# Allocation order and buffer counts: FFN weights and activations at equal addresses modulo 256

## The chip, the cores and the metric

The kernel runs on one core of a Trainium2 chip. The metric is the device time of one execution in microseconds (us); lower is better. Three runs of the kernel before gave 479.50, 479.63 and 480.22 us.

## The reference

One pre-norm transformer layer in fp32, on x of 4 batches x 512 rows x 512 columns:

```python
x = x + attn(layernorm(x), W_q, W_kv, W_o)
x = x + ffn(layernorm(x), gate_w, up_w, down_w, gate_scale, up_scale, down_scale)

# attn: q = x @ W_q.T, kv = x @ W_kv.T, 16 heads of 32
#   qf, kvf = fft over the 32 of a head, each divided by its norm
#   kvf = cumsum(kvf) over the rows;  out = ifft(qf * kvf).real @ W_o.T
# ffn: w -> float8_e4m3 and back for the three weights
#   f = silu((x @ gate_w) * gate_scale) * ((x @ up_w) * up_scale)   # 1536 wide
#   out = (f @ down_w) * down_scale                                  # 512 wide
```

## The kernel before

The order of instructions is written out by hand: each engine runs its instructions in the order of the source, and no scheduler moves them. Tiles come from pools; a pool lays its tiles down in the order in which they are first asked for, so this order and the sizes and buffer counts of earlier tiles set every later tile's address.

**Attention, about 0 to 204 us.** The 2048 rows are 16 chunks of 128. The Fourier transforms are folded into the weights at the start (`fold_in`, `fold_out`). For each chunk TensorE makes the two spectra (pq, L302), a running sum over the rows with a triangle of ones (cum, L357) and the output projection (po, L397). Spectra and projection are full fp32 matmuls. The running sum takes F32R operands, which TensorE handles in one pass: the value is split into a high part kh and a low part kl, and both are multiplied with tri_r and added up. `stats` (L250 to L260) makes mean and 1/deviation of 128 rows with ScalarE and GpSimd, in small tiles "less" (4 buffers) and "dev" (6 buffers). Beside all this ScalarE, VectorE (DVE) and GpSimd (POOL) round the FFN's weights to the float8 grid, a unit of 128 x 1024 at a time (`quant_*`, L196 to L225), into wg, wu and wd.

**FFN, about 204 us to the end.** It has 48 steps: 4 batches x 12 blocks of 128 inner columns. A step n has two parts:

- `inner(n)`, L458 to L485: the gate's 8 and the up's 8 one-pass matmuls into gu (L465). Loaded weights (lhsT) are a 128-column block of wg or wu; the moving operand is 512 columns of yh (high part of the normalized rows) or yl (low part). For each of 4 blocks k, yh and then yl use the same weights. Then ScalarE, DVE make f = silu(gate) * up and split it into fh and fl, which lie in the buffers of kh and kl.
- `down(n - 1)`, L487 to L511: 8 one-pass matmuls into pd (L498). Loaded weights are 128 columns of fh or fl of the step before, the moving operand is 512 columns of wd.

In `behind(n)` stand the remaining weight roundings (first batch alone) and the next batch's rows: statistics, normalization, a turn through DRAM and DVE (`y_turn`, L441 to L452) into the next yh and yl. On the SP queue stand the loads of x, the raw weights, the DRAM turns and the output; ScalarE's queue carries one small transfer per chunk ("row").

The tiles that the change and the prediction speak of, with their byte offset in each partition before and after, and its remainder modulo 256:

| tile | before | mod 256 | after | mod 256 |
|---|---|---|---|---|
| nhalf (64 bytes) | 18624 | 192 | 18656 | 224 |
| table (4 bytes) | 92928 | 0 | 18624 | 192 |
| gus (96 bytes) | 92960 | 32 | 18720 | 32 |
| tri_r | 18688 | 0 | 18816 | 128 |
| wg | 19200 | 0 | 19328 | 128 |
| wu | 43776 | 0 | 43904 | 128 |
| wd | 68352 | 0 | 68480 | 128 |
| dsc | 93056 | 128 | 93056 | 128 |
| yh, yl, wkv, wq, wo (pool "big") | 95104 + 8192 i | 128 | 95104 + 8192 i | 128 |
| x, z, xT, t | from 152448, 2048 apart | 128 | the same | 128 |
| kh, fh (3 buffers) | 187840 + 2048 i | 192 | 188032 + 2048 i | 128 |
| kl, fl (3 buffers) | 193984 + 2048 i | 192 | 194176 + 2048 i | 128 |
| qvT | 220864 | 192 | 221056 | 128 |

A tile of 4 bytes takes 32. All steps inside these tiles (128 columns of fp32 are 512 bytes, 512 columns are 2048) are multiples of 256, so each operand of a matmul has its tile's remainder. Modulo 512 the weights wg, wu, wd lie at 256 before and at 384 after, yh and yl at 384 in both, and fh and fl at 448 before and at 128 after.

Of the kernel before, what the change touches and what calls it, by code (L numbers as in the profile page):

```python
# [7 lines left out]
F32 = mybir.dt.float32  # L8
I32 = mybir.dt.int32
F32R = mybir.dt.float32r  # L10
AF = mybir.ActivationFunctionType
# [4 lines left out]
P = 128  # L16
# [14 lines left out]
def tile_fft_attention_then_fp8_ffn(  # L31
# [38 lines left out]
    nc = tc.nc  # L70
# [4 lines left out]
    MC = FF // P  # L75
# [4 lines left out]
    const = ctx.enter_context(tc.tile_pool(name="const", bufs=1))  # L80
    big = ctx.enter_context(tc.tile_pool(name="big", bufs=7))
    work = ctx.enter_context(tc.tile_pool(name="work", bufs=2))
# [43 lines left out]
    nc.gpsimd.memset(eps, EPS)  # L126
    over = const.tile([P, 1], F32, name="over")
    nc.gpsimd.memset(over, -E4M3_OVERFLOW * DOWN * HUGE)
    nhalf = const.tile([P, H], F32, name="nhalf")
    nc.gpsimd.memset(nhalf, -0.5)  # L130
    tri_r = const.tile([P, P], F32R, name="tri_r")

    wg = const.tile([P, KC, FF], F32R, name="wg")
    wu = const.tile([P, KC, FF], F32R, name="wu")
    wd = const.tile([P, MC, D], F32R, name="wd")

    table = const.tile([P, 1], F32, name="table")
    nc.gpsimd.memset(table, 0.0)
    nc.scalar.activation(table, table, AF.Silu)
    y_all = dram.tile([B, TC, P, D], F32, name="y_all")  # L140
    xn_all = dram.tile([B, TC, P, D], F32, name="xn_all")

# [107 lines left out]
    def stats(src, name):  # L250

        less = work.tile([P, 1], F32, tag="less", name=f"less_{name}", bufs=4)
        rstd = work.tile([P, 1], F32, tag="dev", name=f"dev_{name}", bufs=6)
        each = work.tile([P, D], F32, tag="end", name=f"each_{name}", bufs=1)
        nc.scalar.activation(each, src, AF.Identity, accum_out=less)
        nc.scalar.activation(less, less, AF.Copy, scale=-1.0 / D)
        nc.scalar.activation(each, src, AF.Square, bias=less, accum_out=rstd)
        nc.scalar.activation(rstd, rstd, AF.Identity, scale=1.0 / D, bias=eps)
        nc.gpsimd.tensor_tensor(rstd, rstd, nhalf[:, 0:1], ALU.pow)
        return less, rstd  # L260
# [24 lines left out]
    def x_stats(i):  # L285
        st_x[i] = stats(xt[i], nm(i))
# [128 lines left out]
    def y_stats(b, c):  # L415
        st_y[b, c] = stats(ys[b][:, c, :], f"f{b}_{c}")
# [143 lines left out]
    norms(0, 0)  # L560
    next_parts(1, True)

    gus = const.tile([P, 2, MC], F32, name="gus")
    dsc = const.tile([P, D], F32, name="dsc")
    nc.sync.dma_start(gus[:, 0, :], gate_scale)
    nc.sync.dma_start(gus[:, 1, :], up_scale)
# [185 lines left out]
```

## Time and profile before

| what | value |
|---|---|
| median of 3 runs | 479.63 us |
| the profiled execution | 479.59 us |
| its span on the core | 477.8 us |
| granted TensorE clock, mean | 0.999 |
| weight loads, L302, L465 and L498 | 188 to 190 ns each |
| gu matmuls, L465 | 4 groups of 192 |
| pd matmuls, L498 | 2 groups of 192 |
| DVE busy, 213.8 to 252.8 us | 34.06 of 39.00 us |

How to read it: PE is TensorE's matmuls and PEld its weight loads, which run beside the matmuls before them. A matmul's recorded duration is modelled and reaches past the next one's start, so that the duration of a group's mean (391 to 403 ns for L465) is not what a matmul costs in a row; the distance from one start to the next is. A full fp32 matmul of 512 columns stands in the trace as two records. The page's groups give busy time, mean duration, and the idle time ahead of the group with what ended it. The wait view lists who waited for whom. The timeline gives each instruction's start and duration in us.

### The profile page before, as it was taken

What the parts mean: (1) busy time and instruction counts of PE and PEld (TensorE: products, weight loads), DVE (VectorE), ACT (ScalarE), POOL (GpSimd) and SP (SyncE); (2) the same over time, 40 slices, a digit from 0 to 9 for tenths busy, and PEclk for the clock granted to TensorE, in tenths of its full rate; (3) what the DMA queues carried; (4) which work ended last, traced back from release to release, by engine and by line L of the source; (5) the groups of instructions that cost most, each with busy time, mean ns of one, the idle gap of its engine ahead of it and who ended that gap; (6) DMA issues with size and microseconds to landing.
All of it is one profiled execution on the core that took longest, in us unless ns stands there. A gap on an engine that the chain in (4) does not pass through costs nothing.

```text
span 477.8 us, 5013 instructions
## 1 busy us (share of the span) xinstructions
PE 465.8 (98%) x1736; PEld 314.3 (66%) x1736; DVE 285.8 (60%) x399; ACT 214.8 (45%) x418; POOL 200.9 (42%) x134
## 2 busy tenths in 40 slices
PE   6999999999999999999999999999999999999995
PEld 6534444444444444668888888888888888888883
DVE  1558998888998788768899352333433332522225
ACT  3556475656555864414752325533226433222220
POOL 0247999997987886531432140122210021400002
PEclk9999999999999999999999999999999999999999
DMA  8920414242451200524241040430041420200002
GB/s 277 359 68 24 155 66 155 91 143 93 140 175 58 75 22 22 177 88 154 45 111 22 1 174 3 98 79 0 22 156 37 94 47 0 89 0 1 0 0 88
DMA packets 46152, 40.72 MB, mean 85 GB/s; under 512 B 27696, under 2 KB 28080, under 8 KB 46128
## 3 DMA queue, kind: packets, MB, share of 16 engines
q1 hardware_dynamic: 45744, 40.39, 26.8%
q8 instruction: 13, 0.21, 0.2%
q14 instruction: 11, 0.09, 0.1%
q10 hardware_dynamic: 384, 0.03, 0.1%
HBM read 28.85 MB, written 11.53 MB: 85 GB/s over the span
## 4 chain that ended last, share of the span: by engine, by line
PE 77%; DVE 9%; ACT 5%; POOL 4%; DMA 3%; issue 2%; SPq 0%; DVEq 0%; ACTq 0%
PE gu L465 37%; PE pd L498 19%; PE pq L302 12%; PE po L397 6%; POOL rn L323 3%; DMA row<-end 2%; PE pkv L150 1%; PE pt_v L271 1%; ACT sq L313 1%; ACT end L364 1%; DVE ss L318 1%; DVE qm L217 1%; PE pw L165 1%; PE cum L357 1%; DVE qa L221 1%
## 5 line engine op out<-in xcount | busy, mean ns | idle before, releaser
L323 POOL TENSOR_TENSOR rn<-ss,nhalf 128x16 f32<-128x16 f32 x32 | 107.4, 3358 | 22.3 <-DVE ss L318 22.3
L478 DVE SCALAR_TENSOR_TENSOR f<-gu,gus,g 128x512 f32<-128x512 f32 x48 | 36.0, 750 | 113.7 <-PE gu L465 112.1
L465 PE MATMUL gu<-yh,wg 128*128 128x512 f32 x192 | 77.4, 403 | 0.0
L465 PE MATMUL gu<-yh,wu 128*128 128x512 f32 x192 | 76.6, 399 | 0.0
L498 PE MATMUL pd<-wd,fl 128*128 128x512 f32 x192 | 75.5, 393 | 0.0
L465 PE MATMUL gu<-yl,wu 128*128 128x512 f32 x192 | 75.4, 393 | 0.0
L498 PE MATMUL pd<-wd,fh 128*128 128x512 f32 x192 | 75.3, 392 | 0.0
L465 PE MATMUL gu<-yl,wg 128*128 128x512 f32 x192 | 75.1, 391 | 0.0
L481 ACT CAST fh<-f 128x512 fp32r<-128x512 f32 x48 | 29.8, 621 | 90.7 <-DVE f L478 90.7
L302 PE MATMUL pq<-wkv,xT 128*128 128x512 f32 x128 | 57.7, 594 | 0.6 <-DVE xT L294 0.6
L397 PE MATMUL po<-wo,qvT 128*128 128x512 f32 x128 | 57.6, 593 | 0.0
L302 PE MATMUL pq<-wq,xT 128*128 128x512 f32 x128 | 57.6, 592 | 0.0
L476 ACT ACTIVATE g<-gu,gus 128x512 f32<-128x512 f32 x48 | 33.0, 687 | 54.4 <-PE gu L465 53.6
L510 POOL TENSOR_TENSOR o<-o,ys 128x512 f32<-128x512 f32 x14 | 17.7, 1295 | 83.2 <-DVE o L508 83.2
L483 DVE TENSOR_TENSOR fl<-f,fh 128x512 fp32r<-128x512 f32 x48 | 35.4, 737 | 26.9 <-ACT fh L481 26.8
L302 PEld LDWEIGHTS pq<-wkv,xT 128*128 128x128 f32 x128 | 24.1, 190 | 30.4 <-issue 27.0
L465 PEld LDWEIGHTS gu<-yh,wg 128*128 128x128 f32 x192 | 36.0, 188 | 9.5 <-issue 0.5
L465 PEld LDWEIGHTS gu<-yh,wu 128*128 128x128 f32 x192 | 36.0, 188 | 9.3
L498 PEld LDWEIGHTS pd<-wd,fl 128*128 128x128 f32 x192 | 36.0, 188 | 8.7 <-DVE fl L483 0.2
L465 PEld LDWEIGHTS gu<-yl,wg 128*128 128x128 f32 x192 | 36.1, 188 | 8.4 <-issue 0.5
L498 PEld LDWEIGHTS pd<-wd,fh 128*128 128x128 f32 x192 | 36.0, 188 | 8.3
L465 PEld LDWEIGHTS gu<-yl,wu 128*128 128x128 f32 x192 | 36.1, 188 | 8.0
(84 smaller groups left out, 598.5 us busy)
## 6 DMA issues: line engine op xcount, KB each, us to landing
x<-in_x SPq DMA_DIRECT2D x16, 256.0 KB, 2.8
xT<-in_xT SPq DMA_DIRECT2D x16, 256.0 KB, 2.7
y_all<-x SPq DMA_DIRECT2D x16, 256.0 KB, 2.0
ys<-y_all SPq DMA_DIRECT2D x4, 1024.0 KB, 6.3
out<-o SPq DMA_DIRECT2D x16, 256.0 KB, 2.0
rawf<-in_gate_w SPq DMA_DIRECT2D x3, 1024.0 KB, 6.5
rawf<-in_up_w SPq DMA_DIRECT2D x3, 1024.0 KB, 5.3
rawf<-in_down_w SPq DMA_DIRECT2D x3, 1024.0 KB, 6.2
```

The lines of the kernel that those rows point to most:

```text
L150: nc.tensor.matmul(pw[i][:, j * P : (j + 1) * P], lhsT=r[:, j, i * P : (i + 1) * P], rhs=fwd, start=True, stop=True,)
L165: nc.tensor.matmul(pw, lhsT=inv, rhs=r[:, j, :], start=True, stop=True)
L302: nc.tensor.matmul(pq, lhsT=xTs[i][:, k, :], rhs=w[:, k, :], start=k == 0, stop=k == KC - 1)
L323: nc.gpsimd.tensor_tensor(rns[i, j], sss.pop((i, j)), nhalf, ALU.pow)
L397: nc.tensor.matmul(po, lhsT=qvT[:, k, :], rhs=wo[:, k, :], start=k == 0, stop=k == KC - 1)
L465: nc.tensor.matmul(p, lhsT=w[:, k, m * P : (m + 1) * P], rhs=v[:, k, :], start=k == 0 and v is yhs[b], stop=k == KC - 1 and v is yls[b],)
L476: nc.scalar.activation(g, pgu[0], AF.Silu, scale=gus[:, 0, m : m + 1])
L478: nc.vector.scalar_tensor_tensor(f, pgu[1], gus[:, 1, m : m + 1], g, ALU.mult, ALU.mult)
L481: nc.scalar.copy(fh, f)
L483: nc.vector.tensor_tensor(fl, f, fh.bitcast(F32), ALU.subtract)
L498: nc.tensor.matmul(pds[b][c], lhsT=v[:, c * P : (c + 1) * P], rhs=wd[:, m, :], start=m == 0 and v is fused[n][0], stop=m == MC - 1 and v i ...
L510: add.tensor_tensor(o, o, ys[b][:, c, :], ALU.add)
```

## The change

Three edits in the allocation, none in the computation:

- `table`, the operand of an activation whose use is to load ScalarE's Silu table, is allocated and filled ahead of nhalf instead of behind the weights;
- `gus`, the two scale vectors of the gate and the up matmul, is allocated ahead of tri_r and the weights instead of behind the attention's first chunks; the two DMAs that fill it stay where they were;
- the tag "dev" of `stats` gets 12 buffers instead of 6.

No instruction is added or removed. On GpSimd the fills of table and nhalf change places; on the other engines and on the SP queue the order is the same. With 12 buffers, some of the ScalarE and GpSimd instructions of `stats` (L257, L259) no longer carry a wait for an older reader of their buffer.

```diff
     over = const.tile([P, 1], F32, name="over")
     nc.gpsimd.memset(over, -E4M3_OVERFLOW * DOWN * HUGE)
+
+    table = const.tile([P, 1], F32, name="table")
+    nc.gpsimd.memset(table, 0.0)
+    nc.scalar.activation(table, table, AF.Silu)
     nhalf = const.tile([P, H], F32, name="nhalf")
     nc.gpsimd.memset(nhalf, -0.5)
+
+    gus = const.tile([P, 2, MC], F32, name="gus")
     tri_r = const.tile([P, P], F32R, name="tri_r")
 
     wg = const.tile([P, KC, FF], F32R, name="wg")
     wu = const.tile([P, KC, FF], F32R, name="wu")
     wd = const.tile([P, MC, D], F32R, name="wd")
-
-    table = const.tile([P, 1], F32, name="table")
-    nc.gpsimd.memset(table, 0.0)
-    nc.scalar.activation(table, table, AF.Silu)
...
-        rstd = work.tile([P, 1], F32, tag="dev", name=f"dev_{name}", bufs=6)
+        rstd = work.tile([P, 1], F32, tag="dev", name=f"dev_{name}", bufs=12)
...
-    gus = const.tile([P, 2, MC], F32, name="gus")
     dsc = const.tile([P, D], F32, name="dsc")
     nc.sync.dma_start(gus[:, 0, :], gate_scale)
     nc.sync.dma_start(gus[:, 1, :], up_scale)
```

## Prediction

> **What bounds the kernel now.** I read the page's busy shares and its chain of waits first, then the groups by cost, then TensorE's own waits in the second half, and last the timeline of single matmuls.
>
> ```profile
> PE 465.8 (98%) x1736; PEld 314.3 (66%) x1736; DVE 285.8 (60%) x399; ACT 214.8 (45%) x418; POOL 200.9 (42%) x134
> ...
> PE 77%; DVE 9%; ACT 5%; POOL 4%; DMA 3%; issue 2%; SPq 0%; DVEq 0%; ACTq 0%
> PE gu L465 37%; PE pd L498 19%; PE pq L302 12%; PE po L397 6%; POOL rn L323 3%; DMA row<-end 2%; PE pkv L150 1%; PE pt_v L271 1%; ACT sq L313 1%; ACT end L364 1%; DVE ss L318 1%; DVE qm L217 1%; PE pw L165 1%; PE cum L357 1%; DVE qa L221 1%
> ```
>
> TensorE is the engine of the chain, and two lines of it, gu (L465) and pd (L498), are 56% of the span. Those are the FFN's one-pass (F32R) matmuls, 768 and 384 of them. The wait view for TensorE from 200 us on says whether anything else holds them up:
>
> ```profile
> engine line waited for: us in total, times, longest us
> PE cum L357 <- ACT g L476: 0.2, 1, 0.2
> ```
>
> Nothing does: from about 204 to 472 us TensorE goes from one matmul to the next. So what counts is the spacing from start to start. The timeline (start, duration) around the end of one FFN step and the start of the next:
>
> ```profile
> 263.31 0.39 PE L498 MATMUL pd<-wd,fh 128*128 128x512 f32 x1
> 263.55 0.39 PE L498 MATMUL pd<-wd,fl 128*128 128x512 f32 x1
> 263.77 0.40 PE L465 MATMUL gu<-yh,wg 128*128 128x512 f32 x1
> 264.00 0.39 PE L465 MATMUL gu<-yl,wg 128*128 128x512 f32 x1
> 264.23 0.40 PE L465 MATMUL gu<-yh,wg 128*128 128x512 f32 x1
> 264.47 0.39 PE L465 MATMUL gu<-yl,wg 128*128 128x512 f32 x1
> ...
> 267.27 0.39 PE L465 MATMUL gu<-yl,wu 128*128 128x512 f32 x1
> 267.50 0.39 PE L498 MATMUL pd<-wd,fh 128*128 128x512 f32 x1
> ```
>
> The durations overlap, so they say little; the starts are what to read. Sixteen gu take 263.77 to 267.50, 3.73 us, which is 233 ns each. The trace's start times, in whole ns, show more. In the gu run the spacing alternates 237, 229, 237, 229. At the end of the kernel, where 24 pd follow each other, it repeats 232, 226, 229 (mean 229). The pd that is followed by a gu takes 226 or 227 (263.55 to 263.77 above), in nearly all 44 pairs of that kind that stand in full flow.
>
> For comparison, a record of the attention's full fp32 matmuls (L302, L397) starts every 429 ns. Each is recorded as two, so it is four times 214.5. A one-pass matmul therefore loses 12 to 23 ns somewhere.
>
> **What the Trainium skill says.** "TensorE: Matmul & The Clock Gate", section Back-to-back issue gap, gives N/2.4 + 2.5 ns for a warm matmul, 216 ns at 512 columns. The fp32 records agree (429 / 2 = 214.5), the one-pass matmuls don't (226 to 238, granted clock 1.00). The same page, section Step-by-step, says of the weight load that it "doesn't steal SBUF read bandwidth from the running matmul". And "SBUF — State Buffer", section Who interferes with whom, lets TensorE wait for nobody. The trace speaks against both as far as they go: spacing varies while the weight load beside it stays at 188 ns. No page ties the spacing to addresses, so what follows rests on the trace.
>
> **Where the addresses come in.** The weights that load during a matmul are those of the next one (the weight load's record starts 2 to 4 ns after the matmul). I take each matmul's moving address, the address of the next weights, and their difference modulo 256, from the table of addresses ahead. Within a gu run it is 128. Within a pd run it is 192. From the last gu to the first pd it is 64, and from the last pd to the first gu it is 0, since wd and wg both lie at 0. So the trace already has one kind of matmul with equal addresses, and it is the 226 to 227 one.
>
> A second thing sets the spacing. Start times modulo 13.33 ns are far from evenly spread, and for one difference the spacing is nearly a function of that remainder. For difference 128: remainder 1 to 2 gives 237, remainder 12 gives 229, and each leads to the other, which is the alternation. To compare fairly I take matmuls that start at the same remainder, 9.5 to 10.5: difference 0 gives 226 to 227 (44 matmuls), difference 128 gives 234 (47), difference 192 gives 234 to 237 (47). And 226.7 is 17 times 13.33, so a matmul of difference 0 that starts there ends there: a run of them would stay at 226.7. That it holds for a whole run is my step, as no run of them stands in the trace.
>
> **The change, part by part.**
>
> - *Addresses of the FFN's matmuls.* With gus ahead of the weights, table in front of nhalf and six more small stats buffers, wg, wu, wd, yh, yl, kh, kl all lie at 128 modulo 256: all differences become 0. An FFN step is 16 gu and 8 pd, 3.73 + 1.85 = 5.574 us by start times. At 226.7 it is 24 x 226.7 = 5.441 us, 0.133 less. Times 48 steps: 6.4 us.
>  Bounds for this unknown: the floor is 214.5 for each, 24 x 214.5 = 5.148, -0.426 x 48 = -20.4 us. The other end is that every matmul takes the dearest steady value, 237.5: 24 x 237.5 = 5.700, +0.126 x 48 = +6.0 us. I take -6.4.
> - *Running sum (L357).* 32 one-pass matmuls move from difference 64 to 0 (tri_r and kh, kl). At most 10 ns each, 0.3 us, and partly on the chain only: nothing taken.
> - *fp32 matmuls.* qvT moves from 192 to 128, wo stays at 128. L302 (equal all along) and L397 (unequal before) both have 429 ns, so nothing.
> - *Other engines' operands* move from 192 to 128 as well. ScalarE's cast 128x512 takes 621 ns on f (at 192, L481) and 620 on t (at 128, L451): nothing.
> - *Stats buffers 6 to 12.* Some waits of L257 and L259 for an old reader go away. In ScalarE's and GpSimd's wait views no such wait is among those that cost time: nothing. Nothing is added that could wait.
> - *table ahead of nhalf.* GpSimd's fills are 0.1 us at 0.77 and 0.82 us. ScalarE's table load runs from 0.72 to 2.00 whatever they do, and nhalf is first read at 8.13. Nothing. The queues' order is otherwise the same, DMAs of gus included.
>
> **What is late next.** A faster TensorE comes sooner to what DVE and GpSimd make. The last wu quantization starts at 243.4 and takes at most 1.7; the m = 8 step that reads it starts at 247.2 and gets to those rows 12 matmuls later, 250.0. The last wd ends by 260.8 and is read at 267.7. The next batch's last yl ends at 267.7 and is read at 269.5. By then TensorE is ahead by 10 x 0.133 = 1.3 us, so 1.8 shrinks to 0.5 even if GpSimd kept its clock time; its work follows TensorE's steps, so it mostly moves along. If that cover were gone, it would cost a few tenths once. DVE is at 34.06 of 39.00 us in that stretch and would be at 34.06 of 38.1. The tail after the last pd (471.6 to 477.8: DVE, GpSimd, output DMA) stays.
>
> **Sum.** The profiled execution took 479.59 us: span 477.8 and 1.8 around it. The median of the runs is 479.63, the same. 479.6 - 6.4 = 473.2.
>
> **Rivals.**
>
> 1. *Less: equal means modulo 512.* gu gets difference 0 modulo 512, as in the pair above; pd gets 256 modulo 512, which no F32R pair of the trace has. The nearest is kl of the running sum ahead of po (difference 256, next weights fp32): 226 to 235, mean 232, no better than pd today. Then only gu gains: 16 x (233.1 - 226.7) x 48 = 4.9 us, 474.7; with a worse pattern for gu, 475 to 478.6.
> 2. *More.* The 0-pair is followed by 234 and 224 where 237 and 229 would stand, so part of its gain may show in its neighbours: 5 + 8 = 13 ns in all. If each matmul gained 13 from 233, it would take 220: 24 x 220 = 5.280, 14.1 us less, 465.5. For: two matmuls of unchanged difference are faster after it. Against: that shift follows from the remainder they start at.
> 3. *Nothing happens.* Spacing is the 188 ns weight load plus a fixed 40, whatever the addresses: 479.6. For: the weight load never varies. Against: spacing does, 224 to 238, beside the same weight load.
> 4. *Slower.* Runs of equal addresses don't settle at remainder 10 but in a cycle at the dear end, as gu's remainder 1 to 2 shows 237. The place is the gu and pd runs, the price up to +6.0 us (485.6); it decides from a settled mean above 232.2 ns (5.574 / 24). Against: the only equal pairs are the cheapest at their remainder, and lead back to it.
>
> **How the numbers follow.** Forecast, 472 to 475: 0.42. Rival 1 outside that, 475 to 478.6: 0.20. Rival 2, 465 to 472: 0.18; below 465, towards the floor: 0.04. Nothing: 0.06. Slower: 0.10. A measurement of this kernel can tell about 0.2% (1 us) from no change. Faster by more: 0.84; within: 0.06; slower: 0.10. The range from 465.0 to 478.6 holds 0.80.
>
> **What would show it.** Right: gu and pd spacing near 227 with little alternation, an FFN step of 5.44 us, first half and tail as they were, weight load still 188. Rival 1: gu at 227 and pd at 229 to 232. Rival 2: spacing near 220. Rival 3: 237/229 unchanged. Rival 4: a mean above 232. New entries in TensorE's wait view after 204 us would say that another engine has taken over, which would make the prediction wrong with its spacing right.

## The result and the profile after

The changed kernel takes 473.44 us (median of 4 runs, 472.47 to 474.62) against 479.56 us before, a ratio of 0.9874 with a 95% interval of 0.9846 to 0.9903. The profiled execution took 473.83 us with a span of 471.8 us, 6.0 less than before. Lines of the code are two further down: gu is L467, pd is L500.

From the page of the changed kernel, the busy shares and two lines of the chain:

```profile
PE 459.6 (97%) x1736; PEld 314.4 (67%) x1736; DVE 285.8 (61%) x399; ACT 214.8 (46%) x418; POOL 200.9 (43%) x134
...
PE 77%; DVE 8%; ACT 7%; DMA 3%; issue 3%; POOL 2%; SPq 0%; DVEq 0%; ACTq 0%
PE gu L467 36%; PE pd L500 18%; PE pq L304 12%; PE po L399 6%; DMA row<-end 2%; ACT sq L315 1%; POOL rn L325 1%; PE pkv L152 1%; PE pt_v L273 1%; ACT end L366 1%; PE pw L167 1%; ACT qa L212 1%; DVE kn L328 1%; PE cum L359 1%; DVE kn L342 1%
```

Instruction counts and the busy time of DVE, ScalarE, GpSimd and of the weight loads are the same to 0.1 us. Only the time of TensorE's matmuls shrank, by 6.2 us. Its wait view from 200 us on still shows no one else holding it up:

```profile
PE cum L359 <- ACT g L478: 0.5, 1, 0.5
```

The timeline at the same place as before, the end of one FFN step and the start of the next (start, duration):

```profile
262.75 0.39 PE L500 MATMUL pd<-wd,fl 128*128 128x512 f32 x1
262.97 0.39 PE L467 MATMUL gu<-yh,wg 128*128 128x512 f32 x1
263.20 0.39 PE L467 MATMUL gu<-yl,wg 128*128 128x512 f32 x1
263.42 0.39 PE L467 MATMUL gu<-yh,wg 128*128 128x512 f32 x1
263.65 0.39 PE L467 MATMUL gu<-yl,wg 128*128 128x512 f32 x1
...
266.37 0.39 PE L467 MATMUL gu<-yl,wu 128*128 128x512 f32 x1
266.60 0.39 PE L500 MATMUL pd<-wd,fh 128*128 128x512 f32 x1
266.82 0.39 PE L500 MATMUL pd<-wd,fl 128*128 128x512 f32 x1
```

Sixteen gu take 262.97 to 266.60, 3.63 us or 226.7 ns each, where they took 3.73. The alternation of 237 and 229 is gone: start times in the full flow differ by 225 to 228, in pd too. In the chain of waits (start, us, what) one FFN step was

```profile
286.23 3.73 PE gu L465 x16
289.95 1.85 PE pd L498 x8
```

before, and is now

```profile
284.89 3.63 PE gu L467 x16
288.52 1.81 PE pd L500 x8
```

5.440 us from start to start, against 5.573 before (medians of 43 undisturbed steps). Taken modulo 13.33 ns, the starts of a stretch of some 220 us now lie within 2 ns of one value; before, they were spread over some 12 of the 13 ns.

Where the 6.0 us of the span are: the FFN from its first gu in the chain to the last pd took 267.27 us (204.34 to 471.61) and takes 261.19 (204.78 to 465.97), 6.08 less. The attention ends 0.44 later, of which 0.30 are one transfer of "row" in the chain (5.19 against 5.49 us). The tail after the last pd is 0.34 shorter (6.16 against 5.83). Between the profiles of variants whose attention has the same instructions and buffers but for addresses, its end moves by as much (0.4 us between this one and all_at_0 below), so I put neither down to the change.

### The profile page after: what moved, and what is told of

Read it like the earlier page. It is cut to its first block, busy times and chain, and to the rows that moved or that the text cites. A ratio compares the mean times of both kernels' runs of the same rounds, so it can differ in the third digit from the quotient of the medians.

```text
span 471.8 us, 5001 instructions
## 1 busy us (share of the span) xinstructions
PE 459.6 (97%) x1736; PEld 314.4 (67%) x1736; DVE 285.8 (61%) x399; ACT 214.8 (46%) x418; POOL 200.9 (43%) x134
## 4 chain that ended last, share of the span: by engine, by line
PE 77%; DVE 8%; ACT 7%; DMA 3%; issue 3%; POOL 2%; SPq 0%; DVEq 0%; ACTq 0%
PE gu L467 36%; PE pd L500 18%; PE pq L304 12%; PE po L399 6%; DMA row<-end 2%; ACT sq L315 1%; POOL rn L325 1%; PE pkv L152 1%; PE pt_v L273 1%; ACT end L366 1%; PE pw L167 1%; ACT qa L212 1%; DVE kn L328 1%; PE cum L359 1%; DVE kn L342 1%
## 5 line engine op out<-in xcount | busy, mean ns | idle before, releaser
L467 PE MATMUL gu<-yh,wg 128*128 128x512 f32 x192 | 76.0, 396 | 0.0
L467 PE MATMUL gu<-yh,wu 128*128 128x512 f32 x192 | 74.9, 390 | 0.0
L500 PE MATMUL pd<-wd,fl 128*128 128x512 f32 x192 | 74.8, 390 | 0.0
L500 PE MATMUL pd<-wd,fh 128*128 128x512 f32 x192 | 74.8, 389 | 0.0
L467 PE MATMUL gu<-yl,wg 128*128 128x512 f32 x192 | 74.7, 389 | 0.0
L467 PE MATMUL gu<-yl,wu 128*128 128x512 f32 x192 | 74.7, 389 | 0.0
L304 PE MATMUL pq<-wkv,xT 128*128 128x512 f32 x128 | 57.8, 594 | 0.9 <-DVE xT L296 0.9
L399 PE MATMUL po<-wo,qvT 128*128 128x512 f32 x128 | 57.6, 593 | 0.0
L304 PE MATMUL pq<-wq,xT 128*128 128x512 f32 x128 | 57.6, 592 | 0.0
L304 PEld LDWEIGHTS pq<-wkv,xT 128*128 128x128 f32 x128 | 24.1, 190 | 30.7 <-issue 27.0
L467 PEld LDWEIGHTS gu<-yh,wg 128*128 128x128 f32 x192 | 36.1, 188 | 8.1 <-issue 0.5
L467 PEld LDWEIGHTS gu<-yl,wg 128*128 128x128 f32 x192 | 36.1, 188 | 8.1 <-issue 0.5
L500 PEld LDWEIGHTS pd<-wd,fl 128*128 128x128 f32 x192 | 36.0, 188 | 7.7 <-DVE fl L485 0.2
L500 PEld LDWEIGHTS pd<-wd,fh 128*128 128x128 f32 x192 | 36.0, 188 | 7.5
L467 PEld LDWEIGHTS gu<-yh,wu 128*128 128x128 f32 x192 | 36.1, 188 | 7.4
L467 PEld LDWEIGHTS gu<-yl,wu 128*128 128x128 f32 x192 | 36.1, 188 | 7.4
```

Source lines behind the costliest of these rows:

```text
L304: nc.tensor.matmul(pq, lhsT=xTs[i][:, k, :], rhs=w[:, k, :], start=k == 0, stop=k == KC - 1)
L399: nc.tensor.matmul(po, lhsT=qvT[:, k, :], rhs=wo[:, k, :], start=k == 0, stop=k == KC - 1)
L467: nc.tensor.matmul(p, lhsT=w[:, k, m * P : (m + 1) * P], rhs=v[:, k, :], start=k == 0 and v is yhs[b], stop=k == KC - 1 and v is yls[b],)
L500: nc.tensor.matmul(pds[b][c], lhsT=v[:, c * P : (c + 1) * P], rhs=wd[:, m, :], start=m == 0 and v is fused[n][0], stop=m == MC - 1 and v i ...
```

## The experiments

The theory ahead of them was that of the prediction: in a run of one-pass matmuls the spacing follows from the difference, modulo 256, between the next matmul's weights and the moving operand, and 0 gives 226.7 ns. (Below, a matmul's "own" weights are those that it multiplies with, the "next" ones those of the matmul after it; "settling" is the stretch after a disturbance until the spacing repeats.) Rivals: the gain comes from the fewer waits of `stats` or the early `table` and `gus`; the remainder 128 itself is what is good; smaller steps than 256 count. "Step" below is the median FFN step by start times. A ratio is against the kernel before on the same chip. The runs from d32_96 on are single ones beside a single one of the kernel before, so there I read the spacing and the step, not the time.

**const_only: the early table and gus without the 12 buffers**

```diff
-        rstd = work.tile([P, 1], F32, tag="dev", name=f"dev_{name}", bufs=12)
+        rstd = work.tile([P, 1], F32, tag="dev", name=f"dev_{name}", bufs=6)
```

> The changed kernel with 6 dev buffers, so the weights lie at 128 and fh, fl stay at 192: difference 0 in the gu runs, 64 in the pd runs. Theory (difference of next weights and moving operand modulo 256): gu at 226.7 ns, pd anywhere from 229 to 234, FFN step 5.46 to 5.50 us, 474.1 to 476.0 us. Rival (the fewer waits of stats bring the gain): no gain, 479.6. Rival (table and gus placed early bring it by themselves): all of it, 473.4.

Measured: 477.18 us, ratio 0.9950 (0.9932 to 0.9968), step 5.520. Of 6.1 us gain 2.5 are left (479.69 before, beside it): six buffers of 32 bytes each decide the rest. The time is 1.2 us above the upper end I had expected. The timeline shows where this comes from; it begins with the last pd of a step:

```profile
229.97 0.39 PE L500 MATMUL pd<-wd,fl 128*128 128x512 f32 x1
230.20 0.39 PE L467 MATMUL gu<-yh,wg 128*128 128x512 f32 x1
230.43 0.39 PE L467 MATMUL gu<-yl,wg 128*128 128x512 f32 x1
230.66 0.40 PE L467 MATMUL gu<-yh,wg 128*128 128x512 f32 x1
230.89 0.39 PE L467 MATMUL gu<-yl,wg 128*128 128x512 f32 x1
231.12 0.40 PE L467 MATMUL gu<-yh,wg 128*128 128x512 f32 x1
231.35 0.39 PE L467 MATMUL gu<-yl,wg 128*128 128x512 f32 x1
231.59 0.39 PE L467 MATMUL gu<-yh,wg 128*128 128x512 f32 x1
231.81 0.39 PE L467 MATMUL gu<-yl,wg 128*128 128x512 f32 x1
```

The gu run has difference 0 from its first matmul, yet its first six take 231, 231, 236, 229, 232 and 231 ns, and only then does it settle at 226 to 227. That is 30 ns a step lost to settling. The eight pd (difference 64) alternate between 231 and 236 and lose 52 ns against 226.7. Both parts of the change are needed, and together they give more than the sum of each by itself: only with both have the pd difference 0 too, and a gu run that follows such pd has nothing to settle.

**dev_only: the kernel before with 12 buffers**

```diff
-        rstd = work.tile([P, 1], F32, tag="dev", name=f"dev_{name}", bufs=6)
+        rstd = work.tile([P, 1], F32, tag="dev", name=f"dev_{name}", bufs=12)
```

> The kernel before with 12 dev buffers alone: fh, fl at 128, weights stay at 0. Difference 128 in the gu runs as before, and 128 in the pd runs too (192 before). Theory: gu 233.3 ns as before, pd now the same 237 and 229 alternation, mean 233.3, step 5.60 us, 480.0 to 481.2 us, a little slower than before. Rival (fewer waits of stats): faster, towards 473.4.

Measured: 480.85 us, ratio 1.0022 (1.0012 to 1.0032), step 5.593. The fewer waits bring nothing; pd now has gu's difference and gu's alternation (229, 237), and the step is 0.02 us longer:

```profile
286.66 3.73 PE gu L465 x16
290.39 1.86 PE pd L498 x8
```

**all_at_0: the same differences at another remainder**

```diff
+    const.tile([P, 32], F32, name="pad_a")
     tri_r = const.tile([P, P], F32R, name="tri_r")
```

> The changed kernel with an unused tile of 128 bytes ahead of tri_r, so weights, yh, yl, fh, fl all lie at 0 modulo 256 and not at 128: differences stay 0. Theory: 226.7 ns in gu and pd, step 5.44 us, 473.4 us as the changed kernel. Rival (the remainder 128 itself is what is good): gu and pd back at 229 to 234, 476 to 480 us.

Measured: 473.20 us, ratio 0.9866 (0.9846 to 0.9885), step 5.440. In its chain:

```profile
284.49 3.63 PE gu L468 x16
288.11 1.81 PE pd L501 x8
```

The remainder 128 is not what counts, equality is.

**d64_192, and the sweep d32_96, d160_224, d16_240.** In each, unused tiles ahead of tri_r and behind wd move the weights, or dev gets 16 buffers; in d16_240 the three weights are slices of one tile that start 16 bytes into it. The names give the difference in the gu and in the pd runs. For d64_192:

```diff
+    const.tile([P, 16], F32, name="pad_a")
     tri_r = const.tile([P, P], F32R, name="tri_r")
...
     wd = const.tile([P, MC, D], F32R, name="wd")
+    const.tile([P, 48], F32, name="pad_b")
```

> The changed kernel with unused tiles of 64 and 192 bytes around the weights: weights at 192, the rest at 128. Difference 64 in the gu runs, 192 in the pd runs, 0 from gu to pd and from pd to gu. Theory (0 is special): gu at 229 to 235 ns, pd at 229 to 231 as before, step 5.50 to 5.61 us, 476 to 481 us. Rival (any multiple of 64 that isn't 128 does as well): gu near 227, 474 to 475 us.

Measured: 480.35 us, ratio 1.0013 (1.0006 to 1.0021), step 5.582, as the theory had it, with pd at 231.8 a little above its range. This kernel still has all three edits of the change and adds nothing but unused bytes, and the whole gain is gone: the order of the tiles and the 12 buffers bring nothing of themselves. In its chain:

```profile
286.37 3.73 PE gu L469 x16
290.10 1.86 PE pd L502 x8
```

The sweep's edits, first d32_96 (d160_224 has pads of 40 and 24 elements, and 16 buffers too), then d16_240:

```diff
+    const.tile([P, 8], F32, name="pad_a")
...
+    const.tile([P, 56], F32, name="pad_b")
...
-        rstd = work.tile([P, 1], F32, tag="dev", name=f"dev_{name}", bufs=12)
+        rstd = work.tile([P, 1], F32, tag="dev", name=f"dev_{name}", bufs=16)
```

```diff
-    wg = const.tile([P, KC, FF], F32R, name="wg")
-    wu = const.tile([P, KC, FF], F32R, name="wu")
-    wd = const.tile([P, MC, D], F32R, name="wd")
+    room = const.tile([P, 3 * KC * FF + 64], F32R, name="room")
+    wg, wu, wd = (
+        room[:, 4 + i * KC * FF : 4 + (i + 1) * KC * FF].rearrange("p (k f) -> p k f", k=k)
+        for i, k in enumerate((KC, KC, MC))
+    )
```

> The changed kernel with unused tiles around the weights and 16 dev buffers: difference 32 in the gu runs, 96 in the pd runs. Theory (0 is special, others lie at 229 to 234): both at 229 to 234 ns, step 5.50 to 5.62 us. Rival (the loss grows with distance from 0, by 6.6 ns up to 64): gu at 229 to 231, pd at 233.

Measured: step 5.593; 480.44 us beside 481.28. The gu take 232.3, the pd 234.5, half a nanosecond above the theory's range; the rival's numbers lie below both.

> Difference 160 in the gu runs, 224 in the pd runs. Theory: both at 229 to 234 ns. Rival (loss grows with distance from 0, either way): pd at 227 to 229, gu at 231 to 233. Below 226 in either would say that a better difference than 0 exists.

Measured: step 5.613; 481.48 us beside 481.28. The gu take 234.3, the pd 233.1; the rival's 227 to 229 for pd is missed.

> The three weights moved by 16 bytes inside one tile: difference 16 in the gu runs, 240 in the pd runs. Theory, if equality has to be exact: 229 to 234 ns in both. Rival (only blocks of 32 or 64 bytes count): one or both at 226.7.

Measured: step 5.580; 479.39 us beside 481.28. Neither is at 226.7 (233.2 and 231.0).

All of it in one table, mean spacing in ns over the runs of a step, settling included:

| difference mod 256 | in gu runs | in pd runs |
|---|---|---|
| 0 | 226.7 (after, all_at_0), 228.4 (const_only) | 226.7 (after, all_at_0) |
| 16 | 233.2 | |
| 32 | 232.3 | |
| 64 | 233.1 | 233.1 |
| 96 | | 234.5 |
| 128 | 233.0 (before) | 232.9 |
| 160 | 234.3 | |
| 192 | | 230.7 (before), 231.8 |
| 224 | | 233.1 |
| 240 | | 231.0 |

There is no slope towards 0: 16 bytes off is as dear as 128. A shift of 16 bytes already loses the gain, and no mean here is below 226.7.

Equality is not a price per matmul, though: it is what lets a run settle at 226.7, and until then its matmuls vary like the others. In const_only the gu need six matmuls for it in every step.

**half_load: fewer weights read**

```diff
+                    ends = (k == 0 and v is yhs[b]) or (k == KC - 1 and v is yls[b])
+                    cols = P if ends else P // 2
                     nc.tensor.matmul(
-                        p,
-                        lhsT=w[:, k, m * P : (m + 1) * P],
+                        p[:cols, :],
+                        lhsT=w[:, k, m * P : m * P + cols],
```

> The changed kernel, where 6 of the 8 matmuls of each gu group load and produce 64 columns and not 128; the other half of their products is left out. Theory (the next weights' reads take time from the moving operand's): fewer reads, less loss, these gu at about 214.5 + 12 / 2 = 220.6 ns, weight load shorter than 188. Rival (a fixed price of a one-pass matmul or of a change of weights): they stay at 226.7.

Measured: step 5.480; 475.31 us beside 481.28. The groups of its weight loads (a gu group holds three 64-column loads to one of 128):

```profile
L502 PEld LDWEIGHTS pd<-wd,fh 128*128 128x128 f32 x192 | 36.0, 188 | 7.7
...
L469 PEld LDWEIGHTS gu<-yl,wg 128*64 128x64 f32 x192 | 28.3, 148 | 16.4 <-issue 0.5 <-DVE ss L320 0.2
```

The load of 64 columns takes 134 ns and not 188, and still gu comes out at 229.2 ns on average, dearer than with full loads (226.7). Its eight spacings repeat 226, 236, 229, 224, 227, 234, 231, 226. Both expectations miss: the loss didn't shrink with what is read, and it isn't a fixed price either. Mixing short and full loads breaks the even pattern although all starting addresses are equal, and this run can't tell a saving that the broken pattern hides from no saving.

**own_equal, next_equal, and the same with steps of 64: whose weights?** The prediction took the next matmul's weights as the partner. In these, the four blocks k of wg, wu, yh and yl each start a step further on (their rows get 8 or 16 elements more), so that own and next weights differ; x has 5 buffers to make room. For next_64:

```diff
-    wg = const.tile([P, KC, FF], F32R, name="wg")
-    wu = const.tile([P, KC, FF], F32R, name="wu")
+    wg = const.tile([P, KC, FF + 16], F32R, name="wg")
+    wu = const.tile([P, KC, FF + 16], F32R, name="wu")
...
+    def y_tile(name, first):
+        flat = big.tile([P, KC * D + 64], F32R, tag="big", name=name)
+        steps = flat.rearrange("p (k n) -> p k n", k=KC)
+        return steps[:, :, first : first + D]
...
-            yhs[b] = big_tile(f"yh_{b}", F32R)
-            yls[b] = big_tile(f"yl_{b}", F32R)
+            yhs[b] = y_tile(f"yh_{b}", 0)
+            yls[b] = y_tile(f"yl_{b}", 16)
```

own_64 has 0 in place of the last 16; the other two have steps of 8 elements.

> The changed kernel with the four blocks of wg, wu, yh and yl each 32 bytes further on, and 5 buffers in place of 6 for x. Each gu matmul's moving operand has the remainder of its own weights (difference 0), but half of them (the yl ones) have a difference of 32 or -96 to the next matmul's weights. Theory (the next weights count): gu leaves 226.7, mean 229 to 233 ns, step 5.48 to 5.55 us. Rival (its own weights count): gu stays at 226.7, step 5.44.

Measured: gu 231.4 ns, step 5.533; 480.56 us beside 480.37. Own weights alone don't keep 226.7.

> As the run before, with yl a further 32 bytes on: the moving operand has the remainder of the next matmul's weights in 14 of 16 gu matmuls of a step (the 2 at the end of a group have 128), while half of them (the yl ones) differ by 32 or more from their own weights. Theory (the next weights count): gu near 227 with a disturbance at the two ends, mean 227 to 229. Rival (its own weights count): mean 229 to 233 ns.

Measured: gu 232.3 ns, step 5.570; 482.29 us beside 480.37. The theory's 227 to 229 is missed. As the settling in const_only took six matmuls, two breaks in sixteen could have done that, hence the next two.

> The run next_equal with steps of 64 bytes in place of 32, so that the pattern closes: the moving operand has the remainder of the next matmul's weights in every gu and pd matmul, without a break at the ends of groups, while the yl ones differ by 64 from their own weights. Theory (the next weights alone count, and next_equal missed for its breaks): 226.7 ns all through, step 5.44. Rival (own weights alone, or the whole run has to stay at one remainder): mean 229 to 234 ns in gu.

Measured: gu 231.8 ns, step 5.553; 480.93 us beside 479.80. In its chain:

```profile
288.13 3.71 PE gu L473 x16
291.84 1.84 PE pd L506 x8
```

> The run own_equal with steps of 64 bytes: every moving operand has the remainder of its own weights, and every yl one differs by 64 from the next weights. Theory (own weights alone count): 226.7 ns all through. Rival (next weights alone, or the whole run at one remainder): 229 to 234 ns in gu. If both this run and next_64 are off 226.7, neither pair alone is the rule.

Measured: gu 230.8 ns, step 5.527; 479.14 us beside 479.80. In its chain:

```profile
287.19 3.69 PE gu L473 x16
290.88 1.83 PE pd L506 x8
```

So equality with the next weights alone isn't the rule, nor is equality with its own weights. The theory falls in this point. What the runs support as what lets a run settle at 226.7: each moving operand, its own weights and the next ones all start at one remainder. They don't say whether it is the two equalities together or that the remainder never changes from one matmul to the next. The pd of these four kernels have all their operands at 128, and bear this out: eight of them after a gu run that hasn't settled are too few (228.9 to 231.6 ns on average), but among the 24 pd that end next_64 the spacing is 226 or 227 from the seventh after the pause on.

The times of these four also hold an attention that ends 1.1 to 2.4 us later than in the changed kernel, with its fewer x buffers.

## Why the prediction was right

- *One-pass spacing to 226.7.* Right for gu and pd, to the tenth, and so was the step, 5.441 predicted and 5.440 measured. "A run of them would stay at 226.7" was the step without a trace behind it, and the single remainder of all starts bears it out.
- *The reason given for it.* Right that the address difference modulo 256 sets it (const_only, dev_only, all_at_0), wrong on the partner: "the next weights" alone don't do it (next_64). That the number came out all the same is luck in part: in this change own and next weights all move to one remainder, so the choice of partner could not show. And the 44 pairs it started from had the next weights at the moving operand's remainder, but their own (fl, at 192) not, so by what the later runs support they weren't a case of full equality. In const_only the pd ahead of gu is likewise equal to the next weights and not to its own, and takes 229. The comparison at equal start remainders pointed the right way, but it rested on matmuls at one place of one repeating pattern, and had exceptions: one of the 44 takes 236, and 4 of the matmuls of difference 192 take 225 or 226.
- *The sum, -6.4.* The FFN gave 6.1. One visible part of the rest is at the end: the last FFN step pauses once for fl, for 301 ns from start to start where the kernel before had 260, and the 11 pd after it are spread from 224 to 240 instead of 226.7 (mean 232); only the last of them takes 227. In all_at_0 the same pd settle after 4.
- *Running sum and fp32 matmuls at nothing.* L304 and L399 still start every 429 ns.
- *Buffers, table, other engines' operands at nothing.* dev_only bears out the buffers; d64_192, with all three edits and no gain, bears out the rest; DVE's, ScalarE's and GpSimd's busy times didn't move.
- *What is late next.* Nothing; TensorE waited 0.5 us for ScalarE once after 200 us. (The step that the prediction has start at 247.2 starts at 247.05; nothing hangs on it.)
- *Rivals.* "Equal means modulo 512" falls: pd has 256 modulo 512 and takes 226.7. The kl ahead of po, on which it leaned, has fp32 weights next and wasn't comparable. "More" falls: neighbours don't add 13 ns. "Nothing" and "slower" fall with the measured time; d160_224 and dev_only show that the slower cycles exist (234.3, 232.9). Equal addresses with full weight loads don't repeat such a cycle in any run, but until they settle they can be about as dear (232 over the last 11 pd of the changed kernel).
- *What it took from the Trainium skill.* In the section that it names ("TensorE: Matmul & The Clock Gate", Back-to-back issue gap), 216 ns is the gap of a matmul by itself; for a stream of weight loads and matmuls of 512 columns that section gives about 131 ns, and no run here comes near it (226.7 at best). Nor does a spacing that varies beside a 188 ns load contradict the two statements on reads, as the prediction has it: half_load, which read fewer weights, saved nothing, so it isn't shown that the two reads disturb each other.

Open: why a one-pass matmul with equal addresses still takes 226.7 and not 214.5, and what in the hardware ties 13.33 ns, 256 bytes and the pattern together. half_load shows no loss in proportion to the weights read, and no more than that. Why an equal run takes 4 matmuls to settle in one place and more than ten in another is open too, and steps of less than 16 bytes weren't tried.

## What to carry to other kernels

Where TensorE runs one-pass matmuls back to back, read the distance between starts, not durations: a repeating pattern such as 237, 229 beside an fp32 record at 429 / 2 = 214.5 is a loss that no wait view shows. In a kernel like this one, give weights and moving operands of such runs one remainder modulo 256, in all phases that alternate; a few small tiles or buffers ahead of them decide it, and an unrelated edit to a pool can lose it again. It was worth 1.3% here, and half of the alignment (const_only 0.5%, dev_only -0.2%) brought far less than half of the gain.

## What the runs showed of the hardware

- The spacing of one-pass matmuls of one shape (128x128 by 512 columns), beside weight loads of 188 ns, depends on where operands lie: 226.7 ns in a settled run whose remainders modulo 256 all agree, 230.7 to 234.5 on average in the gu and pd runs otherwise (229 in the 24 pd that end the kernel before), with no gradual approach (16 bytes off: 233.2).
- Equal runs settle after 4 matmuls (the end of all_at_0), six (const_only), or not before the eleventh (the end of the changed kernel), and then stay for the whole FFN if nothing disturbs them; a break of difference between two phases costs anew each time (30 ns a step in const_only).
- A weight load of 64 columns took 134 ns, one of 128 columns 188. The shorter one didn't shorten the spacing (229.2 against 226.7).
